# Row gathers without a bound on their indices: lanes outside the group read row 0, in a two-layer relational attention kernel on one core

## The chip, the cores and the metric

The kernel runs on one core of a Trainium2 chip. The core has five engines with queues of their own: PE (TensorE, matrix products), DVE (VectorE), ACT (ScalarE), POOL (GpSimd) and SP (SyncE, which here only issues transfers). Transfers between the device's memory and the on-chip buffers are carried by 16 DMA engines that all queues share. The metric is device time in microseconds (us) of one execution; lower is better.

## The reference, cut to what matters

The graph has 3,125 nodes with 768 features and 53,125 edges, sorted by destination; each edge has one of three relations. Two attention layers follow each other, the first with four heads of 192, the second with one of 768; then the input is added and each row is normalised. One layer computes:

```python
xr = jnp.einsum('nd,rdf->rnf', x, W)      # a row per node and relation
oi = xr[etype, dst]
oj = xr[etype, src]
alpha = jax.nn.leaky_relu(oi @ q + oj @ k, 0.2)
m = jax.ops.segment_max(alpha, dst, num_segments=n_nodes)
e = jnp.exp(alpha - m[dst])
z = jax.ops.segment_sum(e, dst, num_segments=n_nodes)
a = e / (z[dst] + 1e-16)
out = jax.ops.segment_sum(a[:, :, None] * oj, dst, num_segments=n_nodes) + b
```

The costly part is `oj`: for each edge the row of its source node and relation is fetched from a table of 9,600 rows.

## The kernel before, in words

Nodes are taken in 25 groups of at most 128 neighbouring destinations (`NB`). The edges of a group lie together in the sorted list. The kernel looks at them through a fixed frame: `SL` = 17 columns of 128 lanes (14 in group 0), one edge to a lane, 422 columns in all. A group may have up to 2,176 edges; if it has fewer, the frame's last lanes hold edges of the next group or padding. The list of edges is laid over the frame with a shift of 40 lanes, so that the frame's last 40 edges stand in the first lanes of column 0.

For each group `a_index2` (line 575) writes three tables on VectorE: `dl`, the place of each lane's destination within the group (128 or more where the lane is outside); `ridx`, the row of the table that the lane reads; and `rel`, its relation. For a lane outside, `inv` is 2^20 and is added to the row, which puts the index beyond the table. `gather_rows` (line 485) then fetches one column, 128 rows, by one indirect transfer on POOL's queue. It carries the bound `NP * R - 1` (9,599), and with `oob_is_err=False` a lane beyond it is skipped: its place in the buffer keeps what was there. Groups 0 to 2 are an exception. Their indices are clamped to the last row in a table of their own, `rfirst`, so that each buffer has been filled once with finite numbers before a lane of it is skipped. What a lane outside the group holds does not count: its selector in `picks` (line 477) compares `dl` with 0 to 127 and is zero.

`gather_rows` is called in three places. In phase 1 (`a_gather`, `a_gathers`) and for the last four groups in phase 2 (`key`) it fetches 16 B a lane from `kt1`, the key part of the logits of layer 1. In phase 2 (`gather`) it fetches 3,088 B a lane from `tab1`, the rows of layer 1, into 14 buffers (`share` and `g`). In phase 3 it fetches 3,088 B a lane from `tab2`, the rows of layer 2, into a ring of 44 buffers (`G`).

The phases follow each other. Phase 0 (to some 105 us) prepares the weights and the edge lists. Phase 1 (to some 820 us) multiplies the nodes with the weights of layer 1 (line 742), fills `tab1`, and works out the attention weights of layer 1. Phase 2 (to some 1,760 us) gathers the rows of layer 1, sums them on PE with selectors (line 1028), turns each group's sum and multiplies it with the weights of layer 2 (line 1121), which fills `tab2`. Phase 3 gathers the rows of layer 2, works out its logits (`a_alpha`, line 1282, which reads element 0 of each gathered row), its weights, its sums on PE (line 1340), and the final rows; the last group is summed at line 1384.

The order on each engine is written by hand: every phase has a list of events by step, and each engine executes its instructions in that order. A gather waits until the buffer that it fills has been read, and until the eighth transfer before it on POOL's queue has landed.

Of the kernel before, what the change touches and what calls it, by code (L numbers as in the profile page):

```python
# [12 lines left out]
I32 = mybir.dt.int32  # L13
AF = mybir.ActivationFunctionType
ALU = mybir.AluOpType
# [5 lines left out]
P = 128  # L21
# [11 lines left out]
def _index(ap):  # L33
    return bass.IndirectOffsetOnAxis(ap=ap, axis=0)
# [3 lines left out]
SL = 17  # L38
# [22 lines left out]
def kernel(  # L61
# [21 lines left out]
    R = layers[0]["W"].shape[0]  # L83
    E = src.shape[0]
    NB = (N + P - 1) // P
    NP = NB * P
# [11 lines left out]
    LL = FRONT + E + BACK  # L98
    NK = (NB - 1) * SL + SLF
    V, S, G, T = nc.vector, nc.scalar, nc.gpsimd, nc.tensor  # L100
    OOB = float(1 << 20)

    dram = ctx.enter_context(tc.tile_pool(name="fdram", bufs=1, space=DRAM))
    keep = ctx.enter_context(tc.tile_pool(name="keep", bufs=1))
    first_rows = {0: 0, 1: 1, 2: 2}

    ed_d = dram.tile([4, LL], F32, name="ed_d")
    dr_d = dram.tile([1, LL], BF, name="dr_d")
# [30 lines left out]
    oidx = keep.tile([P, 1], I32, name="oidx")  # L139
    flag = keep.tile([1, 1], I32, name="flag")  # L140
    ridx = keep.tile([P, NB, SL], I32, name="ridx")
    rfirst = keep.tile([P, len(first_rows), SL], I32, name="rfirst")
    dl = keep.tile([P, NB, SL + 1], F32, name="fdl")
    rel = keep.tile([P, NB, SL], F32, name="rel")
    pall = keep.tile([P, NB, SL, H1], F32, name="pall")
# [318 lines left out]
    def slots(b):  # L464
        return SL if b else SLF
# [18 lines left out]

    def gather_rows(to, tab, b, j):

        i = ridx[:, b]
        if b in first_rows:
            i = rfirst[:, first_rows[b]]
        return G.indirect_dma_start(out=to, out_offset=None, in_=tab, in_offset=_index(i[:, j:j + 1]),  # L490
                                    bounds_check=NP * R - 1, oob_is_err=False)

    def start(b, into):

# [56 lines left out]
    def phase1(pre, work, psum, wH, wL, qq):  # L551
# [23 lines left out]
        def a_index2(b):  # L575
            pT = st[b]["pi"]
            c = SL + 1

            p3 = pT[:SHIFT, :3 * c].rearrange("p (r k) -> p r k", r=3)
            V.tensor_copy(p3[:, :, 0], p3[:, :, slots(b)])  # L580
            V.tensor_scalar(dl[:, b, :], pT[:, c:2 * c], 1.0 / BIG, n_all[:, b:b + 1], op0=ALU.mult,
                            op1=ALU.subtract)
            inv = work.tile([P, SL], F32, name="inv", bufs=2)
            V.tensor_scalar(inv, dl[:, b, :SL], float(P), OOB, op0=ALU.is_ge, op1=ALU.mult)
            V.tensor_add(ridx[:, b, :], pT[:, 0:SL], inv)
            if b in first_rows:
                V.tensor_scalar(rfirst[:, first_rows[b], :], ridx[:, b, :], NP * R - 1, None, op0=ALU.min)
            V.tensor_copy(rel[:, b, :], pT[:, 2 * c:2 * c + SL])

            s = st[b]  # L590
            s["lim"] = work.tile([P, 1], F32, name="lim", bufs=2)
            V.tensor_scalar(s["lim"], n_all[:, b:b + 1], float(P), float(N), op0=ALU.add, op1=ALU.min)
# [39 lines left out]
        def a_gather(b, j):  # L632
            gathered[b, j] = gather_rows(kts[b % 3][:, j, :], kt1, b, j).ins
# [180 lines left out]
        for _ in range(4):  # L814
            T.matmul(ahead[0][:, :P], ident, ident, start=True, stop=True)
        d_split(1)
        a_index2(0)
        for j in range(SLF):
            a_gather(0, j)
# [28 lines left out]
        ev = {}  # L848

        chain = ((-6, a_index), (-6, a_index2), (-5, a_gathers), (-5, a_next), (-4, a_next2))  # L850
        turn = [base(b) * STEPS // NE for b in range(NB - LATE)]
        for b, n in enumerate((4, 3, 2, 1)):
# [39 lines left out]
        for n in range(max(ev) + 1):  # L892
            for f, b in ev.get(n, ()):
                f(b)
            b, i = divmod(n, 6)
# [37 lines left out]
    def phase2(work, psum, wH, wL):  # L933
# [19 lines left out]
        def key(b, j):  # L953
            gather_rows(kts[b % 2][:, j, :], kt1, b, j)
# [43 lines left out]
        def gather(k):  # L998
            gather_rows(gs[k % NG], tab1, *in_turn(k))
# [545 lines left out]
    with tc.manual_schedule():  # L1545
        with tc.tile_pool(name="share", bufs=1) as pool:
# [4 lines left out]
            with tc.tile_pool(name="wbuf", bufs=1) as wbuf:  # L1551
                wH = wbuf.tile([P, DT, WW], F32R, name="wH")
                wL = wbuf.tile([P, DT, WW], F32R, name="wL")
                with tc.tile_pool(name="pre", bufs=1) as pre:
                    qq = pre.tile([P, NB, H1, R], F32, name="qq")
                    with tc.tile_pool(name="work0", bufs=1) as work, tc.tile_pool(
                        name="psum0", bufs=1, space=PSUM
# [23 lines left out]
                    with tc.tile_pool(name="work1", bufs=1) as work, tc.tile_pool(  # L1581
                        name="psum1", bufs=1, space=PSUM
# [544 lines left out]
```

## Time and profile before

| | |
|---|---|
| median of three runs | 2508.29 us (2500.16, 2508.29, 2511.01) |
| profiled execution | 2528.77 us, with a span of 2527.0 us |
| PE busy | 1899.4 us (75%) |
| DVE busy | 1199.7 us (47%) |
| POOL busy | 1332.5 us (53%) |
| ACT busy | 383.1 us (15%) |
| moved by DMA | 506.39 MB, of it 331.52 MB on POOL's queue |
| indirect gathers | 1,266, three for each of 422 columns |

The page of the profile gives busy times by engine, the span in 40 slices, the DMA queues, the chain of work that ended last, and the costliest groups of instructions by line. In a group's row, `G<-ftab,ridx x374` names the buffer that is written, what is read, and the number of instructions; after the bar stand the busy time, the mean of one in ns, and the idle time of the engine just before them with what ended it. The line of every gather is L490, the line of the call in `gather_rows`; the gathers are told apart by the buffer they fill (`kt` keys, `share` and `g` layer 1, `G` layer 2). In a timeline, a row is a start, a duration, the instruction, and in brackets the idle time before it. In a table of stretches, each engine has its busy us and its count of instructions, followed by the granted clock of PE, the share of time in which the DMA engines were busy, and GB/s.

### The profile page before, as it was taken

The numbers are of one execution on the slowest core, as the hardware profiler recorded it, in microseconds if no ns is written. First come the engines' busy times: TensorE is split into PE (matmuls) and PEld (weight loads), VectorE is DVE, ScalarE is ACT, GpSimd is POOL, SyncE is SP. The second block draws the span as 40 slices with busy tenths as digits, with TensorE's granted clock in tenths as the row PEclk, the third lists the DMA queues.
The fourth block names the chain that finished last, engine by engine and source line by source line (L and its number), as shares of the span: only waits on it lengthen the run. The fifth ranks groups of instructions, "written<-read, shape, count | busy, mean of one in ns | idle before, by whom it ended". The sixth has DMA issues, their size and how long they took to land.

```text
span 2527.0 us, 40133 instructions
## 1 busy us (share of the span) xinstructions
PE 1899.4 (75%) x13939; PEld 1335.0 (53%) x13939; DVE 1199.7 (47%) x4331; ACT 383.1 (15%) x834; POOL 1332.5 (53%) x1326
## 2 busy tenths in 40 slices
PE   8958987787689688889889889997445444465556
PEld 8746766576568466666666667766122222222223
DVE  7424434333344564555555656652254444445445
ACT  6301111111111011111111111111011111111111
POOL 4355666554350565555555565551656555556552
PEclk9978989898889789899999999999566666676667
DMA  7533444343338766666666768874777777777772
GB/s 228 146 112 112 150 146 149 102 144 113 119 110 307 248 214 206 212 197 211 217 202 213 223 206 253 252 229 169 254 237 269 256 265 239 236 239 246 239 243 102
DMA packets 161765, 506.39 MB, mean 200 GB/s; under 512 B 48027, under 2 KB 57520, under 8 KB 161555
## 3 DMA queue, kind: packets, MB, share of 16 engines
q0 software_dynamic: 81936, 331.52, 42.5%
q1 hardware_dynamic: 69389, 157.78, 17.8%
q10 hardware_dynamic: 10230, 14.43, 1.7%
q8 instruction: 114, 1.87, 0.3%
q14 instruction: 96, 0.79, 0.1%
HBM read 412.74 MB, written 95.69 MB: 201 GB/s over the span
## 4 chain that ended last, share of the span: by engine, by line
PE 51%; issue 20%; another core or an unknown queue 9%; POOL 8%; DVE 7%; DMA 2%; ACT 1%; POOLq 0%; DVEq 0%; SPq 0%; ACTq 0%
PE po L1121 17%; PE po L742 16%; PE acc L1028 9%; POOL G L490 7%; PE acc L1340 3%; DVE selp L482 2%; PE bank L299 1%; DMA G<-ftab,ridx 1%; PE pt L277 1%; PE pt L1095 1%; PE po L414 1%; PE px L714 1%; DVE sT L1251 0%; PE pq L649 0%
## 5 line engine op out<-in xcount | busy, mean ns | idle before, releaser
L490 POOL DMA_INDIRECT kt<-kt,ridx x374 | 393.8, 1053 | 260.6 <-DVE al L672 111.9
L490 POOL DMA_INDIRECT G<-ftab,ridx x374 | 378.2, 1011 | 273.4 <-PE acc L1340 118.2
L1121 PE MATMUL po<-wH,hT 128*128 128x512 f32 (+1 forms) x1500 | 449.9, 384 | 32.4 <-ACT r L1148 17.2
L742 PE MATMUL po<-wH,xT 128*128 128x512 f32 (+1 forms) x1320 | 431.6, 403 | 46.5 <-issue 34.3
L1340 PE MATMUL acc<-G,selp 128*32 128x384 f32 (+1 forms) x2292 | 303.8, 635 | 162.6 <-issue 88.9
L482 DVE TENSOR_SCALAR selp<-frow,fdl,pall 128x32 f32<-128x32 f32 (+1 forms) x1688 | 380.6, 316 | 31.7 <-remote 26.4
L490 POOL DMA_INDIRECT share<-ftab,ridx x239 | 239.9, 1004 | 206.1 <-PE acc L1028 125.4
L1121 PEld LDWEIGHTS po<-wH,hT 128*128 128x128 f32 x1500 | 274.4, 192 | 107.6 <-issue 37.4
L742 PEld LDWEIGHTS po<-wH,xT 128*128 128x128 f32 x1320 | 258.1, 204 | 103.4 <-issue 46.1
L1340 PEld LDWEIGHTS acc<-G,selp 128*32 128x32 f32 x2292 | 127.6, 133 | 312.5 <-issue 191.7
L1121 PE MATMUL po<-wL,hT 128*128 128x512 f32 (+1 forms) x750 | 285.4, 381 | 0.5 <-issue 0.2
L742 PE MATMUL po<-wL,xT 128*128 128x512 f32 (+1 forms) x660 | 261.2, 396 | 11.2 <-issue 10.1
L1028 PE MATMUL acc<-share,selp 128*32 128x193 f32 x3088 | 229.5, 363 | 46.0 <-issue 35.2
L490 POOL DMA_INDIRECT g<-ftab,ridx x135 | 136.0, 1007 | 129.0 <-PE acc L1028 79.5
L1028 PEld LDWEIGHTS acc<-share,selp 128*32 128x32 f32 x3088 | 144.0, 120 | 109.2 <-issue 87.3
L1148 ACT COPY r<-po 128x262 f32<-128x262 f32 (+5 forms) x175 | 71.2, 436 | 713.5 <-PE po L1121 348.4
L1121 PEld LDWEIGHTS po<-wL,hT 128*128 128x128 f32 x750 | 144.4, 193 | 28.4 <-issue 2.0
L742 PEld LDWEIGHTS po<-wL,xT 128*128 128x128 f32 x660 | 134.3, 203 | 39.3 <-issue 16.5
L1028 PE MATMUL acc<-g,selp 128*32 128x193 f32 x1688 | 134.3, 350 | 15.8 <-issue 15.1
L1251 DVE TENSOR_SCALAR sT<-bc,cols 128x512 bf16<-128x512 f32 (+1 forms) x125 | 82.8, 662 | 96.2 <-PE bc L1245 93.2
L1245 PE MATMUL bc<-d,one 1*128 1x512 bf16 (+1 forms) x125 | 48.8, 391 | 96.3 <-DVE sT L1251 65.1
L1028 PEld LDWEIGHTS acc<-g,selp 128*32 128x32 f32 x1688 | 82.6, 116 | 48.5 <-issue 38.6
(309 smaller groups left out, 1963.7 us busy)
## 6 DMA issues: line engine op xcount, KB each, us to landing
ftab<-r SPq DMA_DIRECT2D x74, 386.0 KB
ftab<-share SPq DMA_DIRECT2D x71, 386.0 KB
share<-in_L_gnn_W_dram SPq DMA_DIRECT2D x36, 384.0 KB
w_d<-w2hl SPq DMA_DIRECT2D x18, 768.0 KB
sT<-dr_d SPq DMA_DIRECT2D x25, 534.0 KB
share<-in_x_dram SPq DMA_DIRECT2D x27, 384.0 KB
xb_d<-share SPq DMA_DIRECT2D x25, 384.0 KB
xr<-in_x_dram SPq DMA_DIRECT2D x21, 384.0 KB
```

The costliest lines, as they stand in the source:

```text
L277: T.transpose(pt[:, f, c * P:(c + 1) * P], a[:, (2 * i + f) * P:(2 * i + f + 1) * P], ident)
L299: T.matmul(to, a[:, 2 * i + f, :], t[:, f, :w], start=(n == 0), stop=(n == 2 * DT - 1))
L414: T.matmul(po[g][:, :HALF], a[:, t % 2, :], w[:, t, KQ + r * D + c * HALF:][:, :HALF], start=(t == 0 and n == 0), stop=(t == DT - 1 and n ...
L482: V.tensor_scalar(sel.rearrange("p (t f) -> p t f", f=32), of, dl[:, b, j:j + 1], p, op0=ALU.is_equal, op1=ALU.mult)
L490: return G.indirect_dma_start(out=to, out_offset=None, in_=tab, in_offset=_index(i[:, j:j + 1]), bounds_check=NP * R - 1, oob_is_err=False)
L742: m = T.matmul(po[:, :n], xT[:, s, t, :], w[:, t, KQ + f:KQ + f + n], start=(i == 0), stop=(i == 3 * DT - 1))
L1028: T.matmul(acc[32 * t:32 * t + 32, h // 2, c], sel[:, h, 32 * WINDOW[i].index(t):][:, :32], g[:, h * CW:(h + 1) * CW], start=(i == u[0] an ...
L1121: T.matmul(po[:, :n], hT[:, k, t, :], w[:, t, f:f + n], start=(i == 0), stop=(i == 3 * DT - 1))
L1148: S.copy(o[:, 1 + at - a:1 + at + m], po[:, got - a:got + m])
L1245: T.matmul(bc[:, :n], one, s["d"][:, 4 * i * P:4 * i * P + n], start=True, stop=True)
L1251: V.tensor_scalar(s["sT"][:, 4 * i * P:4 * i * P + n], bc[:, :n], cols[:, b:b + 1], None, op0=ALU.is_equal)
L1340: T.matmul(acc[32 * t:32 * t + 32, c, :HALF + c], st[b, j][:, 32 * WINDOW[j].index(t):][:, :32], gs[:, (base(b) + j) % NG, 1 + c * HALF:][ ...
```

## The change

The gathers lose their bound, and the index of a lane outside the group becomes 0 instead of a number beyond the table. VectorE makes it so: `inv` is now 1 where the lane is inside and 0 where it is not, and the row is multiplied with it. The table `rfirst` and its three minima are gone, and all groups use `ridx`. A lane outside the group is then a lane like any other: it fetches row 0.

```diff
-    OOB = float(1 << 20)
...
-    first_rows = {0: 0, 1: 1, 2: 2}
...
-    rfirst = keep.tile([P, len(first_rows), SL], I32, name="rfirst")
...
     def gather_rows(to, tab, b, j):
 
-        i = ridx[:, b]
-        if b in first_rows:
-            i = rfirst[:, first_rows[b]]
-        return G.indirect_dma_start(out=to, out_offset=None, in_=tab, in_offset=_index(i[:, j:j + 1]),
-                                    bounds_check=NP * R - 1, oob_is_err=False)
+        return G.indirect_dma_start(out=to, out_offset=None, in_=tab, in_offset=_index(ridx[:, b, j:j + 1]))
...
             inv = work.tile([P, SL], F32, name="inv", bufs=2)
-            V.tensor_scalar(inv, dl[:, b, :SL], float(P), OOB, op0=ALU.is_ge, op1=ALU.mult)
-            V.tensor_add(ridx[:, b, :], pT[:, 0:SL], inv)
-            if b in first_rows:
-                V.tensor_scalar(rfirst[:, first_rows[b], :], ridx[:, b, :], NP * R - 1, None, op0=ALU.min)
+            V.tensor_single_scalar(inv, dl[:, b, :SL], float(P), op=ALU.is_lt)
+            V.tensor_mul(ridx[:, b, :], pT[:, 0:SL], inv)
```

## The prediction

> **What bounds the kernel now.** I read the stages first, cutting the span where the work of POOL changes its name: layer 1's row gathers run from 825 to 1706 us, layer 2's from 1760 to 2486 us. The columns are busy us of each engine with its instruction count, then granted clock, DMA share and GB/s.
>
> ```profile
> 825.00:1760.00 935.00, 826.10 (x7220) 616.73 (x7220) 506.73 (x2179) 111.78 (x231) 493.57 (x490) 0.93 0.68 215
> 1760.00:1818.00 58.00, 19.40 (x80) 5.59 (x80) 16.15 (x69) 1.59 (x2) 44.62 (x44) 0.53 0.89 302
> 1818.00:2486.00 668.00, 356.07 (x2746) 149.37 (x2746) 305.19 (x967) 88.20 (x111) 382.16 (x378) 0.66 0.73 243
> 2486.00:2527.00 41.00, 24.26 (x254) 15.70 (x254) 20.31 (x73) 9.21 (x13) 1.03 (x1) 0.83 0.08 30
> ```
>
> In layer 1 PE is busy 826 of 935 us: POOL there waits for PE to free buffers. In layer 2 no engine is full; POOL issues 422 gathers in 726 us. The page's list of groups gives their length, and the waits of POOL within 1818 to 2486 us say what ended its idle time.
>
> ```profile
> L490 POOL DMA_INDIRECT kt<-kt,ridx x374 | 393.8, 1053 | 260.6 <-DVE al L672 111.9
> L490 POOL DMA_INDIRECT G<-ftab,ridx x374 | 378.2, 1011 | 273.4 <-PE acc L1340 118.2
> ```
> ```profile
> POOL G L490 <- PE acc L1340: 129.4, 23, 8.7
> POOL G L490 <- issue: 98.7, 324, 0.3
> POOL G L490 <- remote: 49.8, 22, 2.5
> ```
>
> So 324 of the layer-2 gathers stand back to back with 0.30 us between them (one per 1.305 us), and about twice a group POOL stops for a buffer that PE still reads. A gather moves 128 x 3088 B = 395 KB; at 1.305 us that is 303 GB/s, the 302 GB/s of the first 58 us. Layer 2 is therefore set in part by POOL's pace and in part by the loop through PE; the length of one gather instruction is the number on which most hangs.
>
> **The change, part by part.**
>
> *Lanes that are now read.* I walked the reference's drawn indices (seed 0) through the grouping that the kernel makes. Lanes outside their group: 32 in group 1, none in groups 0 and 2, 398 over eleven of the groups 3 to 23 (at most 40 in column 0 and 24 in column 16), and 370 in group 24 (40 in column 0, 74 in column 14, all 128 in columns 15 and 16). Group 1's 32 are read already, clamped to the last row. So 768 lanes are new: 12 KB in the key gathers (nothing), 2.37 MB in each of the two row gathers.
>
> Layer 1: 2.37 MB at 302 GB/s is 7.9 us if all of it lies bare, and 0 if PE's 826 us cover it; the DMA share of 0.68 leaves room, so I take +1. Layer 2, groups 3 to 23: 398 x 3088 B = 1.23 MB, 4.1 us bare. POOL's pace of 303 GB/s is the cover, if the DMA engines can do more:
>
> ```profile
> 1765.00:1769.00 4.00, 1.32 (x3) 0.33 (x4) 1.50 (x2) 0.00 (x0) 3.09 (x4) 0.50 0.95 340
> ```
>
> They did 340 GB/s in this stretch, so a skipped lane saved time that POOL did not give back. I take +1 of 0 to 4.1. Group 24 is the tail: its last three gathers, and who first needs them:
>
> ```profile
> 2477.82 1.00 POOL L490 DMA_INDIRECT G<-ftab,ridx  x1 [3.55 <-PE acc L1340]
> ...
> 2481.74 1.00 POOL L490 DMA_INDIRECT G<-ftab,ridx  x1 [0.30 <-issue]
> 2483.04 1.00 POOL L490 DMA_INDIRECT G<-ftab,ridx  x1 [0.30 <-issue]
> 2484.34 1.00 POOL L490 DMA_INDIRECT G<-ftab,ridx  x1 [0.30 <-issue]
> ```
> ```profile
> 2503.39 0.19 DVE L1282 TENSOR_TENSOR a<-qe,G 128x17 f32<-128x17 f32 x1 [0.22 <-issue]
> ```
> ```profile
> 2486.00:2489.00 3.00, 0.00 (x0) 0.00 (x0) 2.93 (x10) 1.10 (x1) 0.00 (x0) 0.50 0.01 0
> ```
>
> Today the DMA engines are idle from 2486 us (GB/s 0), because nearly all of columns 14 to 16 is skipped. Now 330 lanes, 1.02 MB, have to land before DVE's logits at 2503.39. At 302 GB/s that is 3.4 us, against 17 us from 2486. I take 0; without that cover it would be 3.4.
>
> *The bound's register.* Each gather loads its bound by a MOVE, and the chain of waits shows one gap with such a step in it and one without:
>
> ```profile
> 2102.64 1.00 POOL G L490
> 2103.64 0.04 issue
> 2103.68 0.03 POOLq L490
> 2103.71 0.23 issue
> 2103.94 0.85 POOL G L490
> ...
> 2107.86 1.00 POOL G L490
> 2108.86 0.30 issue
> 2109.17 1.00 POOL G L490
> ```
> ```profile
> L490 POOLq MOVE  x1266: 29/29/29, 90.5 to 2480.0; - x181
> ```
>
> Both gaps are 0.30 us: POOL's sequencer runs ahead of the gather at work. If every MOVE lay bare in layer 2 the change would give 422 x 0.029 = 12.2 us; the cover is the gather in progress, and I take 0.
>
> *The gather itself without a bound.* No row shows one, so I bound it. Below: the shortest transfer that POOL issues without an index list, 0.53 us against 1.00.
>
> ```profile
> L215 POOL DMA_DIRECT2D dr_d<-share x1: 532/532/532, 52.9 to 52.9; - x1
> L397 POOL DMA_DIRECT2D kt<-kk x9: 577/726/763, 55.5 to 90.5; - x9
> ```
>
> That end can't be used up: at 340 GB/s a gather needs 1.16 us of the DMA engines, so at most 0.14 us of the 1.305 can go before they set the pace. Above: I know of no reason for a longer one, and mirror a third of it, +0.05. Within, I take 0. The rows just shown say why: the gathers at 2483.04 and 2484.34 skip all 128 lanes, the one at 2477.82 (group 24, column 11) skips none, and all three take 1.00 us. What a bound decides about a lane does not show in the instruction's length, and a key gather of 16 B a lane takes as long as a row gather. [...]
>
> *VectorE.* Three minima go, two instructions keep their shape:
>
> ```profile
> L584 DVE TENSOR_SCALAR inv<-fdl x25: 176/177/178, 106.8 to 797.5; 128x17 f32<-128x17 f32 x25
> L585 DVE TENSOR_TENSOR ridx<-pT,inv x25: 175/176/178, 107.0 to 797.7; 128x17 int32<-128x17 f32 x25
> L587 DVE TENSOR_SCALAR rfirst<-ridx x3: 174/176/239, 107.2 to 163.9; 128x17 int32<-128x17 int32 x3
> ```
>
> One operation in place of two, and a product in place of a sum, are the same pass over 17 elements: 0. The three minima are 0.53 us; they stand before the first key gathers, so I take -0.4.
>
> *Order.* Every other instruction of the five engines stands where it stood, with its waits; no queue is passed by anything.
>
> Sum against the profiled execution: 2528.77 + 1 + 1 - 0.4 = 2530.4 us (the span of 2527.0 and 1.8 around it). That execution is 20.5 us above the median of the three runs, 2508.29; the terms carry over, so the forecast is 2510 us: no change that this kernel's measurement tells (0.5%, 12.5 us; the three runs alone lie 10.9 us apart).
>
> **The rivals.**
>
> *Faster: the gather gets shorter.* If POOL spends part of the 1.00 us on comparing each lane with the bound, each back-to-back gather shrinks. For it: an indexed transfer costs 0.3 to 0.5 us more than the plain ones above, and some of it may be the bound. Against: skipped and read lanes cost the same. 44 gathers at the start and 324 after make 368 at POOL's pace. At 0.05 us each that is 18 us, 2492; at the cap of 0.14 it is 52 us, 2458. Layer 1 and the key gathers give little, as POOL waits there.
>
> *Slower: all lanes outside read the same row.* Row 0 is one stretch of 3088 B, asked for up to 128 times by one gather. If the memory serves one row at a lower rate than 128 rows, the last three gathers of each layer come late. The place is the wait at 2503.39, and in layer 1 this one:
>
> ```profile
> 1688.31 1.00 POOL L490 DMA_INDIRECT share<-ftab,ridx  x1 [0.70 <-remote]
> ...
> 1705.70 1.01 POOL L490 DMA_INDIRECT share<-ftab,ridx  x1 [0.69 <-remote]
> ```
> ```profile
> 1716.73 1.52 PE L1028 MATMUL acc<-share,selp 128*32 128x193 f32 x32
> ```
>
> It decides below 47 GB/s in layer 2 (1.02 MB from 2481.74 to 2503.39) and 36 GB/s in layer 1 (1.02 MB from 1688.31 to 1716.73). The trace has a small case of it: column 0 of group 1 reads the last row with 32 lanes, 99 KB, in the gather issued at 1778.95.
>
> ```profile
> 1773.00:1777.00 4.00, 0.11 (x1) 0.00 (x0) 1.01 (x3) 0.00 (x0) 3.08 (x4) 0.50 0.84 279
> 1777.00:1781.00 4.00, 0.58 (x1) 0.00 (x0) 0.28 (x1) 0.00 (x0) 3.08 (x4) 0.50 0.90 315
> 1781.00:1785.00 4.00, 1.34 (x4) 0.34 (x4) 2.09 (x6) 0.00 (x0) 3.09 (x4) 0.50 0.88 298
> ```
>
> Nothing dips while these are under way, so 99 KB fits in some 4 us: at least 25 GB/s, an estimate and no more than a floor. At that floor 1.02 MB takes 41 us: the logits wait until 2523 (+19) and layer 1's sums until 1729 (+12), 31 us, 2541. [...]
>
> *Slower: the unbounded form takes longer*, +0.05 us by the mirrored bound: 18 us, 2528. For it nothing but that no row excludes it.
>
> **How the numbers follow.** Forecast 0.48, with its own range 2500 to 2520. Shorter gathers 0.27 (2452 to 2497). One row served slowly 0.17 (2521 to 2549). Longer gathers 0.08 (2521 to 2530). Hence faster by over 0.5% 0.27, within 0.48, slower 0.25. The range for 8 in 10 leaves out the far half of the shorter gathers and the far half of the slow row: 2475 to 2540.
>
> **What would show it.** Right: gathers of 1.00 us with 0.30 us between them, no MOVE on L490, some 4.7 MB more on POOL's queue, DMA traffic after 2486 us that ends well before DVE's logits of the last group, and no fewer stops of POOL. Wrong: a mean of G's gathers well off 1011 ns, which moves every stage of layer 2 alike; or a DVE wait for the gathers at line 1282's last instruction, or a PE wait before layer 1's last sums, which would be row 0.

## The result, and the profile after

The changed kernel took 2638.47 us (median of four runs, 2635.51 to 2654.60) beside 2509.65 us of the kernel before (four runs, 2500.16 to 2511.24): a ratio of 1.052, with a 95% interval of 1.047 to 1.058. The forecast was 2510 us, so it was wrong: the change cost 129 us. Its profiled execution took 2640.19 us, with a span of 2638.4 us. (The experiments will show that the machine was in one of two conditions, and that the sign of the result belongs to this one.)

The stages of the changed kernel, cut where POOL's gathers change their name; columns as in the prediction.

```profile
108.00:878.00 770.00, 584.67 (x2925) 460.58 (x2923) 278.97 (x860) 110.94 (x350) 353.45 (x355) 0.85 0.41 134
878.00:1828.50 950.50, 829.27 (x7220) 614.66 (x7220) 507.25 (x2192) 112.48 (x231) 466.40 (x490) 0.93 0.66 214
1828.50:2596.50 768.00, 360.96 (x2825) 157.41 (x2826) 320.24 (x1020) 89.81 (x113) 401.82 (x422) 0.64 0.70 236
2596.50:2638.00 41.50, 24.46 (x256) 15.69 (x255) 21.17 (x76) 9.21 (x13) 1.03 (x2) 0.83 0.15 50
```

Logits and keys, before from 108 to 825 us, grew from 717 to 770 us (+53); layer 1 from 935 to 950.5 (+15.5); layer 2 from 726 to 768 (+42); the tail stayed at 41 us. That is the 111 us between the two profiled executions; the one of before lay 19 us above its median, hence 129 us between the medians. No engine got more work: PE's busy time in layer 2 is 361 us against 375.5 before. What changed is the waiting. The groups of gathers on the page after, then what ended POOL's idle time in layer 2, as in the prediction from 58 us after the stage's start:

```profile
L484 POOL DMA_INDIRECT G<-ftab,ridx x422 | 401.8, 952 | 420.6 <-PE acc L1331 168.4
L484 POOL DMA_INDIRECT kt<-kt,ridx x422 | 418.5, 992 | 380.5 <-DVE al L663 146.1
```
```profile
POOL G L484 <- PE acc L1331: 168.4, 22, 8.8
POOL G L484 <- issue: 98.2, 322, 0.3
POOL G L484 <- remote: 74.5, 23, 7.0
```

The gathers became shorter, not longer: 952 ns against 1011. The gap between two of them is still 0.30 us, so they follow one another every 1.254 us instead of 1.305. And yet POOL's stops grew: behind PE's sums from 129.4 to 168.4 us, behind "remote" from 49.8 to 74.5. The same name stands in other engines' waits. Three rows of the whole span, in us, times, and the longest, of before and then of after:

```profile
ACT r L1148 <- remote: 215.8, 35, 15.0
DVE oh L1271 <- remote: 208.8, 24, 29.4
...
ACT share L774 <- remote: 105.5, 17, 24.7
```
```profile
DVE oh L1262 <- remote: 253.7, 24, 13.9
ACT r L1139 <- remote: 246.7, 35, 16.3
...
ACT share L765 <- remote: 133.2, 15, 21.9
```

"Remote" is what the profile says when it finds no cause on this core: the signal that ended the wait came more than 1.5 us after the end of any instruction that could have sent it. By the semaphores in the traces, each of the 209 waits of this name before and of the 197 after was ended by PE's semaphore, so these instructions wait for a result of PE that was long done. That holds for POOL's stops named "remote" too. One group of layer 2 in the timeline after, PE first, then POOL and DVE:

```profile
2155.72 0.61 PE L1256 MATMUL pq<-q2s,sT 128*128 128x9 bf16 x17
2156.62 3.03 PE L1331 MATMUL acc<-G,selp 128*32 128x384 f32 x16 [0.28 <-issue]
2168.70 2.14 PE L1331 MATMUL acc<-G,selp 128*32 128x384 f32 x10 [9.06 <-DVE selp L479]
```
```profile
2163.95 0.95 POOL L484 DMA_INDIRECT G<-ftab,ridx  x1 [0.30 <-issue]
...
2167.73 0.32 DVE L1262 TENSOR_TENSOR oh<-oh,pq 128x153 f32<-128x153 f32 x1 [10.92 <-remote]
2168.08 0.32 DVE L1264 TENSOR_REDUCE qe<-oh 128x17 f32<-128x153 f32 x1
2168.09 0.95 POOL L484 DMA_INDIRECT G<-ftab,ridx  x1 [3.19 <-remote]
```

PE finished the scores `pq` at 2156.33 us. DVE's product `oh`, which waits for no other engine, began 11.4 us later, 2.8 us after the last gather that POOL could issue had ended. The trace also has the signals themselves: between 2155.80 and 2174.38 us it records two updates of PE's semaphore, at 2167.71 and 2167.84, though the work that sends them (`pq` and the sums after it) had ended by 2156.34 and 2159.40. So it is not DVE that started late; the signal came late. POOL's gather at 2168.09 was let go just after, before PE had started its next sums. DVE's selectors follow `oh` on its queue, PE's next sums (2168.70) wait for those, and POOL's gathers after this one wait for PE. In 20 of 24 groups `oh` begins 11.0 to 11.4 us after the scores with the change; before, this was spread over 5.8 to 11.3 us in 22 of 24.

What the prediction named as signs: no MOVE on the gathers' line, and POOL's queue moved 336.27 MB instead of 331.52. The transfers of the tail end well before they are needed, as forecast; the stretch after the last gather, and the last logits, which wait for no gather:

```profile
2596.50:2599.50 3.00, 0.28 (x2) 0.04 (x1) 2.62 (x7) 0.00 (x0) 0.01 (x1) 0.50 0.86 241
```
```profile
2614.99 0.19 DVE L1273 TENSOR_TENSOR a<-qe,G 128x17 f32<-128x17 f32 x1 [0.22 <-issue]
```

### The profile page after: what moved, and what is told of

It is laid out like the page before. It is cut to its first block, busy times and chain, and to the rows that moved or that the text cites. A ratio compares the mean times of both kernels' runs of the same rounds, so it can differ in the third digit from the quotient of the medians.

```text
span 2638.4 us, 38864 instructions
## 1 busy us (share of the span) xinstructions
PE 1898.2 (72%) x13939; PEld 1339.7 (51%) x13939; DVE 1199.1 (45%) x4328; ACT 383.5 (15%) x834; POOL 1259.8 (48%) x1326
## 3 DMA queue, kind: packets, MB, share of 16 engines
q0 software_dynamic: 81936, 336.27, 40.2%
## 4 chain that ended last, share of the span: by engine, by line
PE 34%; issue 15%; another core or an unknown queue 11%; POOL 11%; DVE 3%; DMA 2%; ACT 1%; SPq 0%; POOLq 0%; DVEq 0%; ACTq 0%
PE po L1112 16%; POOL G L484 11%; PE acc L1019 8%; PE po L733 6%; PE acc L1331 2%; DMA G<-ftab,ridx 1%; DVE selp L479 1%; PE pt L1086 1%; ACT r L1139 0%; PE acc L1375 0%; DVE sT L1242 0%; ACT ey L1038 0%; DMA ftab<-r 0%; ACT hT L1093 0%
## 5 line engine op out<-in xcount | busy, mean ns | idle before, releaser
L484 POOL DMA_INDIRECT G<-ftab,ridx x422 | 401.8, 952 | 420.6 <-PE acc L1331 168.4
L484 POOL DMA_INDIRECT kt<-kt,ridx x422 | 418.5, 992 | 380.5 <-DVE al L663 146.1
L733 PE MATMUL po<-wH,xT 128*128 128x512 f32 (+1 forms) x1320 | 437.3, 407 | 60.5 <-issue 34.3
L1331 PE MATMUL acc<-G,selp 128*32 128x384 f32 (+1 forms) x2292 | 290.6, 636 | 205.0 <-DVE selp L479 184.9
L484 POOL DMA_INDIRECT share<-ftab,ridx x272 | 258.7, 951 | 342.6 <-PE acc L1019 170.4
L484 POOL DMA_INDIRECT g<-ftab,ridx x150 | 142.7, 951 | 139.3 <-PE acc L1019 86.2
L1262 DVE TENSOR_TENSOR oh<-oh,pq 128x153 f32<-128x153 f32 x25 | 7.9, 315 | 253.7 <-remote 253.7
```

The source lines that it names most:

```text
L733: m = T.matmul(po[:, :n], xT[:, s, t, :], w[:, t, KQ + f:KQ + f + n], start=(i == 0), stop=(i == 3 * DT - 1))
L1262: V.tensor_mul(oh, oh, s["pq"][:, :SL * R * 3].rearrange("p (j k) -> p j k", j=SL))
L1331: T.matmul(acc[32 * t:32 * t + 32, c, :HALF + c], st[b, j][:, 32 * WINDOW[j].index(t):][:, :32], gs[:, (base(b) + j) % NG, 1 + c * HALF:][ ...
```

## The experiments

Theory A: the shorter period of the gathers lengthens the waits for PE's results, because these signals get through only when the gathers let up. Theory B: the reads of row 0 do it, by their place or their bytes. Theory C: the register move ahead of each bounded gather lets the signals through. Theory D came up on the way: where there are no such waits, layer 2 is as long as its gathers take.

The runs under one heading ran on one chip, beside runs of the kernel before on that chip. Its median was 1944 to 1947 us beside E1 to E8, E10 to E12 and E18, and 2517 to 2598 us beside E9 and E13 to E17. I call the longer times condition I (the result was taken in it) and the shorter ones condition II. The condition is no property of a chip: E14 and E15 met a chip in condition I (2598 us), and E18 met the same chip in condition II (1944 us).

### E1 to E4: bound, row, move, memset

```diff
 E1 (to the changed kernel)
-        return G.indirect_dma_start(..., in_offset=_index(ridx[:, b, j:j + 1]))
+        return G.indirect_dma_start(..., in_offset=_index(ridx[:, b, j:j + 1]),
+                                    bounds_check=NP * R - 1, oob_is_err=False)
 E2
-            V.tensor_mul(ridx[:, b, :], pT[:, 0:SL], inv)
+            V.tensor_scalar(ridx[:, b, :], pT[:, 0:SL], float(NP * R - 1), 0.0, op0=ALU.min, op1=ALU.max)
 E3, ahead of each gather
+        G.reg_mov(pace, NP * R - 1)
 E4, behind each gather (tick is one element)
+        G.memset(tick, 0.0)
```

> The changed kernel with the bound put back into every gather; the outside lanes keep index 0, so that they still read row 0 and the bytes stay those of the changed kernel. Theory A (what was lost is lost because the gathers without a bound follow one another every 1.254 us instead of 1.305 us, and results of TensorE reach VectorE, ScalarE and GpSimd only when the burst of gathers lets up): the period goes back to about 1.305 us, and the time to that of before, 2500 to 2520 us. Theory B (what was lost is lost through the reads of row 0, by their place or their bytes): about 2638 us, as with the change, and the waits for TensorE's results stay as long as there.

> The changed kernel, no bound, but the outside lanes read the row that stands in their own place of the edge list instead of row 0: the same bytes, spread over the table. Theory A: nothing changes against the changed kernel, about 2638 us. Theory B in its form that row 0 is crowded: clearly less than 2638 us, towards 2510 us; in its form that the extra bytes alone cost: about 2638 us, and then it is E1 that tells A from B.

> The changed kernel with one register move on GpSimd ahead of each gather, as the bounded gather had it; the gather itself stays without a bound. Theory A: the move hides in the 0.304 us between two gathers, the period stays 1.254 us, and the time stays near 2638 us. Theory C (the move itself, an instruction on GpSimd between two gathers, is what lets the other engines' signals through): back to 2500 to 2520 us. Theory B: about 2638 us.

> The changed kernel with a memset of one element on GpSimd behind each gather. Theory A: the period grows by the memset, some 0.1 to 0.3 us, to 1.3 us or over; the waits for TensorE's results shorten, and although GpSimd does more, the time falls below 2638 us, to between 2490 and 2600 us. Theory B: GpSimd's extra work comes on top, 2638 us or more.

Measured, beside a before of 1944.5 us (13 runs): E1 1948.6 us, ratio 1.002 (1.001 to 1.003); E2 1924.2 us, 0.990 (0.988 to 0.991); E3 1925.1 us, 0.991 (0.989 to 0.993); E4 1928.3 us, 0.992 (0.990 to 0.993). No theory had this: the kernels without a bound were faster, and all times lay far below those of the result (the kernel before by 565 us). No wait in these traces is put down to "remote". In E3 the move did not reach the program (its page counts 38,864 instructions, like the changed kernel), so E3 is a repeat of the changed kernel, and C stayed untried. E4's memset of 98 ns fitted into the gap, and the period stayed at 1.251 us.

Two things follow in condition II. Rows of their own (E2) and row 0 (E3) differ by 0.9 us: row 0 costs nothing that reaches the end. Nor is it served more slowly: after the last gather of layer 2, when most of what is still to come is row 0, the packets of the gathers (6,176 B, two rows each) take 235 ns in the median in E3, as in the rest of the stage. And the form without a bound is worth 1.2% against the same indices with it (E3 against E1).

### E5 and E6: the changed kernel and E1 again

> The changed kernel once more, unaltered. On the chip of E1 to E4 the kernel before takes 1944 us instead of 2509 us, and the same three kernels without a bound are 0.8 to 1.0% faster than it. If the loss of 5.2% belongs to the changed program, it shows here as a ratio of about 1.05 wherever this lands; if it belongs to the slower of the two conditions (waits of the other engines on TensorE's results, 0.7 us for one register instruction of SyncE, before at about 2509 us), then the ratio is 0.99 beside a before of about 1944 us, and 1.05 only beside a before of about 2509 us.

> E1 once more, beside the changed kernel itself: bound kept, outside lanes on row 0. Beside a before of about 1944 us: 1.002 times before, as in E1. Beside a before of about 2509 us: theory A (the faster succession of gathers costs, in the slower condition) gives about 1.00; theory B (the reads of row 0) gives about 1.05.

Measured beside 1946.8 us: the changed kernel 1926.2 us, 0.990 (0.988 to 0.992); E1's kernel 1950.2 us, 1.002 (1.001 to 1.003). The loss belongs to condition I and not to the program alone. No trace of the kernel before was taken in condition II; E1 stands in for it here. Layer 2 in condition II, of the changed kernel (E5) and of E1, and their groups:

```profile
1363.00:1892.00 529.00, 326.19 (x2924) 158.27 (x2928) 329.44 (x1086) 92.31 (x116) 400.45 (x421) 0.73 0.95 343
```
```profile
1366.00:1918.00 552.00, 335.60 (x2956) 163.86 (x2956) 330.75 (x1065) 92.32 (x116) 423.00 (x422) 0.72 0.94 330
```
```profile
L484 POOL DMA_INDIRECT G<-ftab,ridx x422 | 401.4, 951 | 181.3 <-issue 102.7
```
```profile
L484 POOL DMA_INDIRECT G<-ftab,ridx x422 | 423.1, 1003 | 181.2 <-issue 107.6
```

422 gathers of 1.251 us are 528 us, of 1.303 us 550 us: layer 2 is the gathers and nothing else, and the DMA engines are busy 94 to 95% of it. The granted clock of PE is lower in condition I (0.64 against 0.73 in layer 2 of the changed kernel), but with it PE works 361 us there against 326, and the stage takes 239 us more: a slower PE does not explain it.

### E7 and E8: the bound left out in layer 2 alone, and everywhere but there

```diff
+        bound = dict(bounds_check=NP * R - 1, oob_is_err=False) if tab is not tab2 else {}   # E8: if tab is tab2
-        return G.indirect_dma_start(..., in_offset=_index(ridx[:, b, j:j + 1]))
+        return G.indirect_dma_start(..., in_offset=_index(ridx[:, b, j:j + 1]), **bound)
```

> The changed kernel with the bound kept in the gathers of logits and of layer 1 (844 of 1266) and left out in layer 2 alone (422). Beside a before of about 1945 us, theory D (only in layer 2 do the gathers follow one another without a break, so that 0.05 us less for each shortens the stage; elsewhere TensorE sets the pace): 422 times 0.05 us is 21 us less, about 1925 us, the whole gain of the changed kernel. Rival (each of the 1266 gathers saves something on the path): a third of the gain, about 1938 us. Beside a before of about 2509 us, theory A gives +42 us (what layer 2 lost there), theory B about +45 us.

> The other half of E7: no bound in the gathers of logits and of layer 1, the bound kept in layer 2. Beside a before of about 1945 us, theory D: no gain, 1945 to 1951 us like E1. Rival: two thirds of the gain, about 1933 us. Beside a before of about 2509 us, theory A gives +68 us (what the stages up to layer 2 lost there).

Measured beside 1944.1 us: E7 1926.7 us, 0.991 (0.989 to 0.993); E8 1945.1 us, 1.0005 (0.9996 to 1.0015). Theory D holds: the gain comes from the 422 gathers of layer 2, and the other 844 save little that reaches the end (E8's ratio lies 0.0015 below E1's, some 3 us, and their intervals overlap).

### E9: four memsets behind each gather, in condition I

```diff
 (to E4; tick is now 128x64)
-        G.memset(tick, 0.0)
+        for _ in range(4):
+            G.memset(tick, 0.0)
```

> E4 with four memsets of 128x64 behind each gather instead of one of one element. In E4 the memset of 98 ns lay within the 0.304 us between two gathers and the period stayed 1.25 us. Four of 0.1 to 0.2 us no longer fit: the period grows to between 1.35 and 1.75 us. Beside a before of about 1945 us, theory D (layer 2 is as long as its 422 gathers take) gives 422 times the growth over 1.251 us on top of 1928 us: 1970 to 2140 us. Rival (something else paces layer 2 with some room): less than half of that. Beside a before of about 2509 us, theory A gives less than the 2638 us of the changed kernel, although GpSimd works longer.

Measured: 2878.0 us beside 2587.5 us, ratio 1.110 (1.103 to 1.118). Time and period both lay above what was expected: the period became 1.89 us in the logits and in layer 2 and 2.30 us in layer 1, and the chain of waits now belongs to POOL (44%). But condition I's mark was gone: not one wait is put down to "remote", and `oh` begins 0.4 us after the scores in nearly every group of layer 2. That was the first sign for A.

### E10 to E12: two memsets

```diff
 E12 (to E9)
-        for _ in range(4):
+        for _ in range(2):
```

> The changed kernel beside E11 and E12. Beside a before of about 1945 us: 0.99, as in E5. Beside a before of 2500 us or more (E9 met 2587 us): 1.04 to 1.06, as in the result, with 11 us between the last matmul of the scores L1256 and the product L1262 that waits for it, in most groups of layer 2.

> E1: bound kept, outside lanes on row 0. Beside a before of about 1945 us: 1.002. Beside a before of 2500 us or more, theory A (the other engines' signals are held up while gathers follow one another too closely, so the period decides, 1.305 us with the bound and 1.254 us without): 0.99 to 1.01. Theory B (row 0): 1.04 to 1.06.

> E9 with two memsets instead of four behind each gather: the period should be 1.4 to 1.6 us (1.89 us with four). In E9 hardly a wait of the kind of the result was left, but 1.89 us for each gather bound every stage. Theory A beside a before of 2500 us or more: most of the waits gone with far less work on GpSimd, so faster than the changed kernel and than before, 2050 to 2450 us, ratio 0.80 to 0.97. If waits and period are unconnected: slower than the changed kernel there. Beside a before of about 1945 us, theory D: layer 2 longer by 422 times the growth of the period over 1.251 us, 63 to 147 us, so 1990 to 2075 us.

Measured beside 1945.1 us: the changed kernel 1925.4 us, 0.990 (0.988 to 0.991); E11 1948.7 us, 1.002 (1.001 to 1.003), both as before; E12 2362.2 us, 1.214 (1.212 to 1.216), far above the 1990 to 2075 expected. The period in layer 2 came out at 1.48 us, and the stage grew by 163 us where 422 times the growth of the period is 96; in layer 1 it came out at 1.88 us. This is POOL in E18, with memsets of one element in layer 1: the pair takes 0.23 us, and the gather behind it starts another 0.62 us later:

```profile
1012.23 0.94 POOL L485 DMA_INDIRECT share<-ftab,ridx  x1 [0.56 <-issue]
1013.17 0.23 POOL L487 MEMSET tick<- 1x1 f32 x2
1014.02 0.96 POOL L485 DMA_INDIRECT share<-ftab,ridx  x1 [0.62 <-issue]
```

So these spacers are dear where there is nothing to gain: E12 is what the spacing costs in condition II.

### E13: one memset, in condition I

```diff
 (to E9)
-        for _ in range(4):
+        for _ in range(1):
```

> The changed kernel with one memset of 128x64 behind each gather. In E9 and E12 one such memset took 0.16 to 0.2 us, against the 98 ns of the memset of one element in E4, which did not change the period of 1.251 us; the period should come out between 1.25 and 1.35 us, near the 1.305 us of the kernel before. Beside a before of 2500 us or more: theory A 0.97 to 1.01, theory B 1.05 or more. Beside a before of about 1945 us, theory D: layer 2 longer by 422 times the growth over 1.251 us, up to 42 us, so 1925 to 1970 us.

Measured: 2634.3 us beside 2517.3 us, 1.045 (1.037 to 1.052). The period came out at 1.277 us, halfway between the two kernels, and the waits stayed:

```profile
ACT r L1143 <- remote: 279.3, 33, 16.4
DVE oh L1266 <- remote: 250.6, 23, 19.6
```

By its number this fits B. It does not tell, since the period of before was not reached; but an instruction on POOL between two gathers is not by itself what lets signals through, which speaks against C, though the move itself was never tried.

### E14 and E15: E1's and E12's kernels, in condition I

> E1 again, bound kept and outside lanes on row 0. Beside a before of 2500 us or more: theory A (the gather without a bound, by its shorter period) 0.99 to 1.01; theory B (the reads of row 0) 1.04 to 1.06. Beside a before of about 1945 us: 1.002.

> E12 again, period 1.48 us in the bursts. On a chip with a before of 1945 us it took 2362 us with no waits for signals. Beside a before of 2500 us or more: theory A, if 1.48 us is enough for the signals, 2360 to 2480 us, ratio 0.92 to 0.97, faster than before; if it is not enough, or if the spacing has nothing to do with it, 2650 us or more.

Measured beside 2597.6 us (13 runs): E14 2598.5 us, 1.001 (0.998 to 1.005); E15 2371.2 us, 0.914 (0.907 to 0.921). E14 reads row 0 as often as the changed kernel and moves the same bytes, and costs nothing. So B falls in condition I too, with one reserve: the changed kernel itself did not run beside E14, where condition I was harsher than in the result (2598 against 2510 us). E15 has no bound either and is 8.6% faster than before, almost as fast as the same kernel in condition II (2362 us). One group of layer 2 in E15's timeline:

```profile
1957.98 0.62 PE L1260 MATMUL pq<-q2s,sT 128*128 128x9 bf16 x17
1957.99 0.95 POOL L485 DMA_INDIRECT G<-ftab,ridx  x1
...
1958.89 1.75 PE L1335 MATMUL acc<-G,selp 128*32 128x384 f32 x8 [0.29 <-issue]
1958.94 0.38 POOL L487 MEMSET tick<- 128x64 f32 x2
1959.38 0.32 DVE L1266 TENSOR_TENSOR oh<-oh,pq 128x153 f32<-128x153 f32 x1 [0.30 <-PE pq L1260]
1959.46 0.95 POOL L485 DMA_INDIRECT G<-ftab,ridx  x1
```

`oh` starts 0.8 us after the scores, in the middle of a burst of gathers. Its waits over the whole span, in E14 and in E15:

```profile
ACT r L1140 <- remote: 391.5, 44, 18.0
DVE oh L1263 <- remote: 221.9, 21, 23.7
```
```profile
DVE oh L1266 <- remote: 5.2, 3, 2.4
```

### E16 and E17: the spacing between, in condition I

```diff
 (to E12; tick: E16 one element, E17 128x32)
-    tick = keep.tile([P, 64], F32, name="tick")
+    tick = keep.tile([1, 1], F32, name="tick")     # E17: [P, 32]
```

> The changed kernel with two memsets of one element (98 ns each in E4) behind each gather: by the gaps of E12 and E13 a period of about 1.33 us. Theory A beside a before of 2500 us or more: if the waits end below 1.33 us, 2070 to 2200 us, ratio 0.80 to 0.86; if 1.33 us is still too short, 2500 us or more. Beside a before of about 1945 us, going by E12 (437 us more for 0.227 us of period): about 2085 us.

> Two memsets of 128x32 behind each gather, between E16 and E12: a period of about 1.40 us. Theory A beside a before of 2500 us or more: 2190 to 2300 us, ratio 0.84 to 0.90, if the waits end below 1.40 us; 2450 us or more if not. Beside a before of about 1945 us, going by E12: about 2210 us.

Measured beside 2587.9 us: E16 2445.5 us, 0.944 (0.938 to 0.949); E17 2390.2 us, 0.926 (0.920 to 0.932). Both took longer than forecast. Layer 1 ran at 1.80 and 1.86 us a gather, and in E16 the logits took 716 us, with 323 us of waits named "remote" left in them. The waits shrank step by step; `oh` in E16:

```profile
DVE oh L1266 <- remote: 42.5, 16, 12.2
```

All in one table. "Beside" is the median of the kernel before that ran along, which tells how harsh the condition was. The period is the median in layer 2; "layer 2" runs from its first to its last gather; "over" is this less 421 periods, what the stage loses beside its gathers; "`oh`" is the median time from the end of the scores to the start of `oh`; "remote" is the sum of all waits of that name over all engines, a floor, since a wait whose signal is missing from the trace stands under "issue".

| condition, kernel | beside, us | bound | period, us | layer 2, us | over, us | `oh`, us | remote, us | ratio to before |
|---|---|---|---|---|---|---|---|---|
| I, changed | 2510 | no | 1.254 | 767 | 239 | 11.2 | 1159 | 1.052 |
| I, E13 | 2517 | no | 1.277 | 768 | 230 | 11.4 | 1174 | 1.045 |
| I, E14 | 2598 | yes | 1.303 | 759 | 211 | 11.2 | 1227 | 1.001 |
| I, before | 2510 | yes | 1.306 | 724 | 174 | 8.4 | 1006 | 1 |
| I, E16 | 2588 | no | 1.334 | 658 | 97 | 2.5 | 425 | 0.944 |
| I, E17 | 2588 | no | 1.425 | 675 | 75 | 1.9 | 273 | 0.926 |
| I, E15 | 2598 | no | 1.479 | 692 | 70 | 0.7 | 128 | 0.914 |
| I, E9 | 2587 | no | 1.892 | 866 | 70 | 0.4 | 0 | 1.110 |
| II, changed (E5) | 1947 | no | 1.251 | 529 | 2 | 0.4 | 0 | 0.990 |
| II, E1 | 1945 | yes | 1.303 | 550 | 2 | 0.4 | 0 | 1.002 |
| II, E18 | 1944 | no | 1.330 | 638 | 78 | 0.4 | 0 | 1.170 |
| II, E12 | 1945 | no | 1.478 | 692 | 70 | 0.4 | 0 | 1.214 |

E12 and E15 are the same program and lose the same 70 us of layer 2 in both conditions: that is the memsets' own price. E16 and E18 (below) have the same memsets in layer 2 and lose 97 us in condition I and 78 in II. What condition I adds falls from some 240 us of layer 2 to 209 (E14), 19 (E16) and nothing (E15) as the period goes from 1.25 to 1.48 us, and beside a before of 2510 to 2517 us the order by period holds too (239, 230, 174 us). E15 to E17 have the same number of instructions and differ in the length of the memsets alone, and the waits still fall with the period. In the logits, where a gather moves 2 KB, the sum named "remote" goes, in the order of the table, 385 us (changed), 419 (E13), 380 (E14), 346 (before), 323 (E16), 216 (E17), 108 (E15), 0 (E9); so the waits do not need the bytes that the gathers move in layer 2. That is what theory A says.

Three reservations. No gather without a bound was run at 1.305 us, so the form and the period are told apart by the row of E13 to E17 and not at one point. In layer 2 the largest step lies between 1.303 us without memsets and 1.334 us with two, and how much of it is the period and how much the memsets is not separated. And in E9 and E15 to E17 layer 1 was spaced wider than layer 2.

### E18: a spacing for each stage

```diff
 (to E12)
-            G.memset(tick, 0.0)
+            G.memset(tick if tab is kt1 else tick[:1, :1], 0.0)
```

> Two memsets of 128x64 behind each gather of the logits (period 1.48 us), two of one element behind those of layer 1 and layer 2 (1.33 us). Beside a before of 2500 us or more, the stages of E15 and E16 added: 108 + 579 + 870 + 50 + 658 + 39, about 2305 us, ratio 0.88 to 0.91. If the waits of layer 1 and layer 2 hang on more than their own spacing: 2350 us or more. Beside a before of about 1945 us, going by E12 with less in layers 1 and 2: 2080 to 2200 us, slower than before.

Measured: 2273.1 us beside 1943.6 us, 1.170 (1.167 to 1.172), above the range given, again by layer 1 (925 us from its first gather to layer 2's, at 1.80 us a gather, where E5 takes 732). It met condition II, so whether it beats E15 in condition I was not seen.

Of the versions that ran in both conditions none beat the kernel before in both: in II the changed kernel is the fastest (0.990), in I E15 (0.914).

## Why the prediction was wrong, step by step

*The gather itself without a bound: 0.* This step failed. The gather is some 0.05 us shorter without the bound (medians of 949 against 1002 ns in layer 2, means of 952 against 1011). The inference was faulty: gathers that skip all lanes and gathers that skip none take the same 1.00 us, and I concluded that the bound costs nothing. Equal lengths said that the outcome for a lane is free, not that the bound is. By itself this step misses by some 20 us and towards faster; it does not make the result. The sign "a mean of G's gathers well off 1011 ns" came up.

*The rival "the gather gets shorter".* Its 0.05 us was right, and in condition II so was its price: 18 us forecast, 20.6 us measured (E5). The place was right too: layer 2 has the whole gain (E7), and there all 422 gathers count instead of the 368 that stood back to back in the profile of before. In condition I its sign was wrong.

*The loop through PE.* This is the step behind the 129 us. I wrote that layer 2 is set in part by POOL's pace and in part by the loop through PE, and took the second part as fixed, as if POOL's stops would stay as long when the gathers come faster. That failed: they hang on POOL's pace. Over and above the gathers, layer 2 lost 174 us before and 239 us after, 65 us more where the shorter gathers save 22. I also read POOL's stops as waits for a buffer that PE still reads; the 22 of them named "remote" ended with a signal of PE that was late. The row "remote" stood in the prediction with its 49.8 us, and the page's chain of waits gave 9% to "another core or an unknown queue", in a program that has one core. I put no price on either and asked for no rival there. The same holds for the stages before layer 2, to which the prediction gave nothing and +1 us: the logits and layer 1 lost 53 and 15.5 us, and the waits for late signals grew there from 346 to 385 and from 402 to 431 us. Nothing in the profile of before gave the sign of the dependence; that the stop exists, and that it ended when a burst of gathers did, was to be read in it.

*Lanes that are now read: +1 and +1, tail 0.* About right: with the bound kept, the indices of the changed kernel cost 0.2% in condition II (E1, 4 us), and in condition I nothing that the interval of E14 tells from none. *The rival of row 0*: wrong in condition II (E2 against E3), and in I as far as E14 tells. The upper end of that rival's range, 2549 us, has behind it a rate for one row that no run shows; what the runs showed is the stretch after the last gather, most of it row 0, which moved 241 GB/s over 3 us, and packets no slower than in the rest of the stage (235 ns, E3).

*The bound's register: 0; VectorE: -0.4.* The gap between gathers stayed at 0.30 us without the MOVE, as forecast. What VectorE saves is too small to be told.

## What to carry to other kernels

A shorter instruction on one engine is not a shorter stage (in the result 0.05 us less a gather, and 42 us more in layer 2): ask what happens to the waits between its bursts, and whether their length was measured at this pace only. Waits that a profile puts down to something outside, in a program with nothing outside, are time that no row explains, and belong in the sum as a term of either sign. And before a few per cent are explained by the program, run both kernels in another place or at another time: here the same change is 1.0% faster or 5.2% slower.

## What the runs showed of the hardware that I had not expected

The same program takes 1945 us or 2500 to 2600 us, with the same chip in both conditions at different times. They part at the first gather, which starts at 108 us in both; in condition I no wait before it is named "remote". In condition I register instructions of SyncE, which wait for nothing, take up to 0.73 us on the line shown here; the changed kernel in condition I and in condition II (E5), with least, median and most in ns:

```profile
L498 SPq FUSED_REGOPS  x121: 3/152/727, 160.2 to 2290.7; - x121
L498 SPq SEQ_ASSERT  x121: 3/18/710, 160.4 to 2292.1; - x121
```
```profile
L498 SPq FUSED_REGOPS  x121: 152/152/171, 136.5 to 1670.5; - x121
L498 SPq SEQ_ASSERT  x121: 18/18/26, 136.7 to 1670.8; - x121
```

What holds the signals up is open. Those that the traces show late are PE's alone (all 209 waits named "remote" before and all 197 after). Counted in the traces, the landings of transfers left 27,920 semaphore events in E5, 27,980 in E12 and 27,988 in E1, but 12,295 before and 12,121 after the change, and 18,521 in E15: in condition I events are missing from the record, and roughly the more the longer the waits. E9, with no wait named "remote", still lacks some (23,537). Whether the recording itself delays the engines, or both suffer from a third thing, no run here shows.

In GpSimd's gathers, one memset of 98 ns fits into the 0.30 us between two of them without changing the period of 1.251 us (E4). Two of one element do not: with them the period came out at 1.33 us in layer 2 and at 1.80 us in layer 1 (E16).
